# Ordering the first Winograd product by contraction chunk, and moving the second quad's four weight sums from VectorE to GpSimd

## The chip, the cores and the metric

The kernel runs on one core of a Trainium2 chip. The metric is the device time of one execution in microseconds. Three runs of the kernel before gave 762.72, 764.22 and 764.67, a median of 764.22 us.

The core's engines are TensorE (matmuls; PE in the profile, its weight loads PEld), VectorE (DVE), ScalarE (ACT), GpSimd (POOL) and SyncE (SP, which here only issues DMAs). Each engine has its own instruction stream and executes it in order; engines wait for each other and for DMAs through semaphores.

## The reference, cut to what matters

The kernel computes a transformer layer in float32: a cross-attention and a feed-forward part with low-rank experts, each with a residual. There are 16 batches of 64 tokens, so 1024 tokens, a model width of 512 and 32 heads of width 128. Only the key projection is touched:

```python
q = (hidden_q @ Wq).reshape(b, lq, h, dh)
k = (hidden_kv @ Wk).reshape(b, lk, h, dh)
v = (hidden_kv @ Wv).reshape(b, lk, h, dh)
score = jnp.einsum('bqhd,bkhd->bhqk', q, k) * scale + position_bias
...
return ctx @ Wo
```

`hidden_kv` is `ctx_4096` (1024 x 512) and `Wk` is 512 x 4096. The keys of four heads, 1024 x 512 numbers, are called a quad here; there are eight quads (`NQ`).

## The kernel before, in words

**Exact products.** A float32 operand is split into two parts that TensorE can take: `hi`, a rounded copy that ScalarE makes (L70, `nc.scalar.copy`, shown as CAST), and `lo`, the rest, which VectorE makes as source minus `hi` (L71, shown as TENSOR_TENSOR). A product is three matmuls, hi by hi, lo by hi and hi by lo (`mm3`, L256 to L260; in the profile all have L259). In the profile `gh` and `gl` are the two parts of a weight block, and `t1h`, `t1l`, `t6h` and so on those of a token block.

**Seven products instead of eight.** The projection of a quad is cut into 2 by 2 blocks (token half by model-width half against model-width half by column half) and done by Winograd's scheme with seven block products, numbered 1 to 7 and run in the order 1, 2, 6, 5, 7, 4, 3 (`ORDER`, L37). Product 1 multiplies plain blocks; product 6 multiplies a sum of weight blocks by a sum of token blocks; and so on.

- Weights (`class Weights`, L153 to L173) needs four sums of weight blocks, each one instruction over 128 x 512 numbers at L161: `s1` = a21 + a22 and `s2` = s1 - a11 when product 6 is prepared, `s3` = a11 - a21 for product 7, `s4` = a12 - s2 for product 3. The engine that makes them is an argument (`eng`). They come from a pool of four buffers (`sum`).
- Tokens (`class Tokens`, L119 to L146) needs four differences of token blocks, at L132, each in two instructions.

**One block product** has two column blocks (k = 0, 1), each of 128 columns and with its own PSUM bank, and a contraction of 256 in two chunks (kc = 0, 1) of 128. `mm_weights` (L262) does for one column block both chunks, six matmuls; the loop in `winograd` (L243 to L254) goes over the column blocks. After the last matmul of a column block, `post` evicts it or adds banks up: for product 1 a ScalarE copy `u` (L220), for product 2 a VectorE add `c` = `u` + PSUM bank (L223), and so on; a result block `c` is stored by SP (L340).

**The start of the program.** The first two quads, q = 0 and q = 1, go side by side (L363 to L399), because both need the same token blocks. For each product number, the code prepares quad 0's weights, the tokens and quad 1's weights, then does quad 0's and quad 1's product. SP loads what they need in the order of L299 to L309: the upper weight blocks and the first half of the tokens, by contraction chunk, come first; then the second half of the tokens; last the lower weight blocks a21 and a22 of quad 0 and of quad 1. Before the first real product, 18 small matmuls over zeros run on TensorE (L353). The operations ahead of the very first product are written out by hand (L354 to L361): chunk 0 of the tokens is split first, chunk 1 follows when its load is there.

**What sets the order.** TensorE's order is the order of the code (`manual_schedule`, L350). In this part of the program the order on VectorE, ScalarE, GpSimd and SP is set at build time by a planner, except for the lines L354 to L361. An order once set is fixed: an engine does not overtake a waiting instruction.

**What comes after.** At L400 to L408 the other key quads and the value products ("o" stages, `OctWeights`, four column blocks each, weight sums on VectorE at L193) follow; then queries and attention (L427 on), where GpSimd makes the query weights' sums (L430, L161) and adds the mask to the position bias (L461); then the feed-forward part. GpSimd also makes the token differences of the queries (L580, L132). The six banks of the PSUM pool `psp` and the two of `pss` are reused in turn, so a later product waits until an earlier one has been read out.

Of the kernel before, what the change touches and what calls it, by code (L numbers as in the profile page):

```python
# [36 lines left out]
ORDER = (1, 2, 6, 5, 7, 4, 3)  # L37
# [10 lines left out]
def xattn_ffn_kernel(ctx: ExitStack, tc: tile.TileContext, x, ctxT, wq, wk, wv, wo, fside, mask,  # L48
                     base_wT, base_b, arT, router_b, lora_b, expert_map, out):
    nc = tc.nc  # L50
# [12 lines left out]
    def bank(k=None):  # L63
        return psp.tile([P, 512], F32, tag="ps", name="ps")

    def blk(tag, name, dt=F32, shape=(P, 512)):
        return pools[tag].tile(list(shape), dt, tag=tag, name=name)
# [41 lines left out]
    with ExitStack() as actx:  # L109
# [6 lines left out]
        def small_bank(name):  # L116
            return pss.tile([P, 512], F32, tag="s", name=name)
# [92 lines left out]
                    self.make(i)  # L210
                return self

        def winograd(mm, n, emit, yzbank=bank, order=ORDER):

            xb, zb, yb, u, u2, u3 = ({} for _ in range(6))

            def post(i, k):
                if i == 1:
                    u[k] = blk("sn", "u")
                    nc.scalar.copy(u[k], xb[k])  # L220
                elif i == 2:
                    c = blk("ob", "c11")
                    nc.vector.tensor_tensor(c, u[k], zb[k], ALU.add)  # L223
                    emit(0, 0, k, c)
                elif i == 6:
                    u2[k] = blk("sn", "u2")
                    copied[:] = [nc.scalar.copy(u2[k], xb[k])]
                elif i == 7:
                    u3[k] = blk("sn", "u3")
                    copied[:] = [nc.scalar.copy(u3[k], xb[k])]  # L230
                    c = blk("ob", "c22")
                    nc.vector.tensor_tensor(c, u3[k], yb[k], ALU.add)
                    emit(1, 1, k, c)
                elif i == 4:
                    c = blk("ob", "c21")
                    nc.scalar.copy(c, xb[k])
                    emit(1, 0, k, c)
                elif i == 3:
                    c = blk("ob", "c12")
                    nc.vector.tensor_tensor(c, u2[k], yb[k], ALU.add)  # L240
                    emit(0, 1, k, c)

            for i in order:  # L243
                for k in range(n):
                    if i == 1:
                        xb[k] = bank()
                    elif i == 2:
                        zb[k] = yzbank(k)
                    elif i == 5:
                        yb[k] = yzbank(k)  # L250
                    b = xb if i in (1, 6, 7, 4) else zb if i == 2 else yb
                    mm(i, k, b[k], i in (1, 2, 5))
                    post(i, k)
                yield i  # L254

        def mm3(o, stat, mov, first, last):  # L256
            (sh, sl), (mh, ml) = stat, mov
            for n, (a, b) in enumerate(((sh, mh), (sl, mh), (sh, ml))):
                nc.tensor.matmul(o, lhsT=a, rhs=b, start=first and n == 0, stop=last and n == 2,  # L259
                                 skip_group_check=True)  # L260

        def mm_weights(t, g):  # L262
            def mm(i, k, o, first):
                for kc in range(2):
                    mm3(o, [a[:, kc, k * P:(k + 1) * P] for a in g[i]], [b[:, kc] for b in t[i]],
                        first and kc == 0, kc == 1)
            return mm
# [15 lines left out]
        def gran4(r, eng):  # L283
            return Weights(r[0, 0], r[0, 1], r[1, 0], r[1, 1], 256, eng)
# [8 lines left out]
        rks = {}, {}  # L293
# [44 lines left out]
        def emit_k(q):  # L338
            def emit(i, j, k, c):
                stored[:] = [nc.sync.dma_start(out=kd[4 * q + 2 * i + k][:, j * HALF:(j + 1) * HALF], in_=c)]  # L340
            return emit
# [4 lines left out]
            return emit  # L346

        tc_ = Tokens(cT, nc.vector)
        gs = [gran4(r, nc.vector) for r in rks]
        with tc.manual_schedule(engines={nc.tensor.engine}):  # L350
            warm = small_bank("warm")
            for _ in range(WARM):
# [1 line left out]
            with tc.manual_schedule(engines={nc.tensor.engine, nc.vector.engine, nc.scalar.engine}):  # L354
# [5 lines left out]
                nc.vector.tensor_tensor(lo[:, 0], cT[:, 0, 0:HALF], hi[:, 0].bitcast(F32), ALU.subtract)  # L360
                split(hi[:, 1], lo[:, 1], cT[:, 1, 0:HALF])  # L361
            gs[1].make(1)
            both = [winograd(mm_weights(tc_, gs[q]), 2, emit_k(q), yz) for q, yz in  # L363
                    enumerate((bank, lambda k: small_bank("yz")))]

            def keys_of(q, g):
                xn = {}
                for i in winograd(mm_weights(tc_, g), 2, emit_k(q)):
                    if 3 <= q < 7:
                        t = 2 * (q - 3)  # L370
                        if i in (1, 6):
                            xn[i] = x_tile(t + (i == 6))
                        if i in (6, 7):
                            with tc.issue_after(copied[-1].ins):
                                norm(sm, *([a] for a in xn[1 if i == 6 else 6]))
                        elif i == 5:
                            x_turn(t, xn[1][0])
                        elif i == 3:
                            x_turn(t + 1, xn[6][0])
# [20 lines left out]
            for n, (q, kind) in enumerate(stages[:-1]):  # L400
                load(n + 2)
                ops[n + 1].all()
                if kind == "k":
                    keys_of(q, ops[n])
                else:
                    for i in winograd(mm_oct(tc_, ops[n]), 4, emit_oct(q),
                                      lambda k: bank() if k < 2 else small_bank("yz")):
                        pass  # L408
                if n == 1:
                    with tc.issue_after(stored[-1].ins):  # L410
                        nc.sync.dma_start(out=m8, in_=mask)
                        nc.sync.dma_start(out=emi, in_=expert_map.partition_broadcast(P))
                        nc.sync.dma_start(out=rb, in_=router_b.partition_broadcast(P))
                    nc.vector.tensor_scalar(maskb, m8, -1.0, BIG, ALU.add, ALU.mult)
                    nc.vector.tensor_reduce(valid, m8, AX.X, ALU.max)
                    nc.vector.tensor_copy(emf, emi)
                    for e in range(E):
                        nc.vector.tensor_scalar(oneh[:, e, :], emf, float(e), 2.0, ALU.is_equal, ALU.mult)
# [188 lines left out]
            for p in range(NP):  # L607
                steps = ("QSQQQQQQt" if p == 0 else "SQQQPQQOOQOhOQOOOO" if p + 2 < NP else
                         "SQQQPQQOQQfSeeOOOOOhh" if p + 1 < NP else "PooOOOOOOO")
                n = 0  # L610
# [130 lines left out]
    def mm(o, a, b, start=False, stop=False):  # L741
        nc.tensor.matmul(o, lhsT=a, rhs=b, start=start, stop=stop, skip_group_check=True)  # L742
# [8 lines left out]
    def ffn_route(pa):  # L751
        lg = fs2.tile([P, NR], F32, tag="lg", name="lg")
        nc.vector.tensor_tensor(lg, pa[:, E * R:NAR], rb, ALU.add)
        nm = fs2.tile([P, 1], F32, tag="nm", name="nm")
        nc.vector.tensor_reduce(nm, lg, AX.X, ALU.max, negate=True)
        sme = fs2.tile([P, 1], F32, tag="sme", name="sme2")
        nc.scalar.activation(lg, lg, AF.Exp, bias=nm, accum_out=sme)
        return pa, lg, sme
# [58 lines left out]
    with tc.manual_schedule(engines=fixed):  # L817
# [10 lines left out]
        r = ffn_route(pas[0])  # L828
# [3 lines left out]
    with tc.manual_schedule(engines=fixed | {nc.vector.engine}):  # L832
        for t in range(NT):
# [4 lines left out]
            if t + 1 < NT:  # L838
                r = ffn_route(pas[t + 1])
            n = 1 if t else 2  # L840
# [55 lines left out]
```

## Time and profile before

| what | value |
|---|---|
| median of three runs | 764.22 us (762.72 to 764.67) |
| the profiled execution, span from first to last instruction | 761.7 us |
| mean granted TensorE clock in it | 0.999 |
| instructions | 16780 |
| the first matmul of the key projection | 4.73 us |
| first GpSimd instruction behind the making of constants | 111.88 us |

The profile is of one execution, and the page gives no time of its own for it besides the span. The median of the runs lies 2.5 us above the span; what lies around the span belongs to a run's time and not to the profile.

The views used below are these. The page's first part gives each engine's busy time and share of the span. The chain of waits is followed back from the last instruction, at each step to what released it. The list of waits tells which engine and line waited for which, with total, number and longest. A timeline has, for each instruction, the start, the length in us, the engine, the line, the operation, output `<-` inputs with shapes, and in square brackets the idle time ahead of it and what ended that. A VectorE instruction is listed with its full length, and the next one may start a little before that length is over, so that instructions 0.60 us apart are listed with 0.68. A table of windows has, for each stretch, its length, the busy time of PE, PEld, DVE, ACT and POOL with the number of instructions, the granted clock (PEclk), the busy share of the DMA engines and GB/s.

### The profile page before, as it was taken

What the parts mean: (1) busy time and instruction counts of PE and PEld (TensorE: products, weight loads), DVE (VectorE), ACT (ScalarE), POOL (GpSimd) and SP (SyncE); (2) the same over time, 40 slices, a digit from 0 to 9 for tenths busy, and PEclk for the clock granted to TensorE, in tenths of its full rate; (3) what the DMA queues carried; (4) which work ended last, traced back from release to release, by engine and by line L of the source; (5) the groups of instructions that cost most, each with busy time, mean ns of one, the idle gap of its engine ahead of it and who ended that gap; (6) DMA issues with size and microseconds to landing.
All of it is one profiled execution on the core that took longest, in us unless ns stands there. A gap on an engine that the chain in (4) does not pass through costs nothing.

```text
span 761.7 us, 16780 instructions
## 1 busy us (share of the span) xinstructions
PE 752.5 (99%) x6154; PEld 624.9 (82%) x6154; DVE 565.8 (74%) x1076; ACT 412.0 (54%) x1157; POOL 194.8 (26%) x271
## 2 busy tenths in 40 slices
PE   8999999999999999999999999999999999999998
PEld 6888888888788888877888888888888888888898
DVE  7986567666655776869778777787778777878975
ACT  5654444444444445667645565456645765474361
POOL 0000008108820693223220222022211232010330
PEclk9999999999999999999999999999999999999999
DMA  6685647465735446466554465436544564462011
GB/s 255 229 285 186 205 157 229 147 218 179 224 130 187 156 126 225 142 222 217 189 158 149 138 199 167 142 120 201 174 141 134 180 185 140 125 199 84 1 57 56
DMA packets 84946, 126.79 MB, mean 166 GB/s; under 512 B 11776, under 2 KB 35072, under 8 KB 84864
## 3 DMA queue, kind: packets, MB, share of 16 engines
q1 hardware_dynamic: 80624, 123.56, 49.9%
q0 software_dynamic: 4096, 2.11, 1.2%
q8 instruction: 48, 0.79, 0.5%
q14 instruction: 34, 0.28, 0.1%
q10 hardware_dynamic: 144, 0.06, 0.0%
HBM read 83.74 MB, written 35.65 MB: 157 GB/s over the span
## 4 chain that ended last, share of the span: by engine, by line
PE 91%; DVE 3%; POOL 2%; DMA 2%; issue 1%; ACT 0%; SPq 0%; DVEq 0%; ACTq 0%; POOLq 0%
PE ps L259 73%; PE yz L259 5%; PE ps L742 5%; PE ps L517 4%; PE pss L470 4%; POOL xT L333 1%; DMA cT<-in_ctxT 1%; DMA so<-in_wo 0%; DMA xT<-xb 0%; DVE bs L708 0%; DVE gl L71 0%; PE pt L104 0%; DVE s L161 0%; DVE ol L71 0%; POOL st L711 0%
## 5 line engine op out<-in xcount | busy, mean ns | idle before, releaser
L481 ACT ACTIVATE p<-p,nm 128x64 f32<-128x64 f32 x256 | 85.9, 339 | 33.3 <-DVE nm L475 31.0
L534 DVE TENSOR_TENSOR acc<-acc,ps 128x512 f32<-128x512 f32 x128 | 86.8, 681 | 21.2 <-PE ps L259 20.4
L259 PE MATMUL ps<-wh,ol 128*128 128x512 f32 x256 | 99.9, 390 | 0.8 <-DVE ol L71 0.8
L259 PE MATMUL ps<-wh,oh 128*128 128x512 f32 x256 | 100.1, 391 | 0.0
L259 PE MATMUL ps<-wl,oh 128*128 128x512 f32 x256 | 99.7, 389 | 0.0
L70 ACT CAST gh<-s 128x512 fp32r<-128x512 f32 (+1 forms) x128 | 64.4, 514 | 56.0 <-PE ps L259 45.7
L333 POOL DMA_DIRECT2D xT<-xb x128 | 69.7, 552 | 84.9 <-DVE xb L330 80.7
L71 DVE TENSOR_TENSOR gl<-s,gh 128x512 fp32r<-128x512 f32 (+1 forms) x128 | 72.0, 566 | 23.2 <-ACT gh L70 23.1
L161 POOL TENSOR_TENSOR s<-rq 128x256 f32<-128x256 f32 x32 | 25.3, 790 | 238.9 <-DMA rq<-in_wq 190.1
L71 DVE TENSOR_TENSOR ol<-ps,oh 128x512 fp32r<-128x512 f32 x64 | 39.9, 683 | 31.5 <-ACT oh L70 31.3
L70 ACT CAST gh<-raw 128x512 fp32r<-128x512 f32 x48 | 29.8, 623 | 52.8 <-PE yz L259 36.1
L259 PEld LDWEIGHTS ps<-wh,ol 128*128 128x128 f32 x256 | 48.1, 188 | 11.4 <-DVE ol L71 1.6
L259 PEld LDWEIGHTS ps<-wl,oh 128*128 128x128 f32 x256 | 48.1, 188 | 10.0
L259 PEld LDWEIGHTS ps<-wh,oh 128*128 128x128 f32 x256 | 48.0, 188 | 10.0
L71 DVE TENSOR_TENSOR gl<-raw,gh 128x512 fp32r<-128x512 f32 x48 | 35.1, 731 | 27.9 <-ACT gh L70 20.7
L461 POOL TENSOR_TENSOR bm<-bm,maskb 128x512 f32<-128x512 f32 x32 | 42.4, 1348 | 36.6 <-DMA bm<-in_fside 36.6
L481 ACT ACTIVATION_READ_ACCUMULATOR p<-p,nm 128x1 f32 x256 | 48.6, 190 | 0.0
L565 DVE TENSOR_TENSOR q<-u,ps 128x512 f32<-128x512 f32 x48 | 32.8, 683 | 20.4 <-PE ps L259 16.0
L70 ACT CAST oh<-ps 128x512 fp32r<-128x512 f32 x64 | 33.2, 590 | 11.0 <-PE ps L517 11.0
L70 ACT CAST gh<-rq 128x256 fp32r<-128x256 f32 x48 | 19.5, 406 | 36.0 <-PE ps L259 32.1
L517 PEld LDWEIGHTS ps<-pt,v 64*64 64x64 f32 x2048 | 31.9, 135 | 5.7 <-issue 5.6
L554 ACT COPY u<-ps 128x512 f32<-128x512 f32 x48 | 27.9, 581 | 15.9 <-PE ps L259 8.8
(258 smaller groups left out, 1986.2 us busy)
## 6 DMA issues: line engine op xcount, KB each, us to landing
kd<-c SPq DMA_DIRECT2D x64, 256.0 KB, 2.6
vd<-c SPq DMA_DIRECT2D x64, 256.0 KB, 2.8
kT<-kd SPq DMA_DIRECT2D x64, 256.0 KB, 3.9
v<-vd SPq DMA_DIRECT2D x64, 256.0 KB, 3.7
raw<-in_wk SPq DMA_DIRECT2D x32, 256.0 KB, 4.0
raw<-in_wv SPq DMA_DIRECT2D x32, 256.0 KB, 4.3
rq<-in_wq SPq DMA_DIRECT2D x32, 256.0 KB, 4.1
bm<-in_fside SPq DMA_DIRECT2D x32, 256.0 KB, 4.5
```

The lines of the kernel that those rows point to most:

```text
L70: first = nc.scalar.copy(hi, src)
L71: return first, (lo_eng or nc.vector).tensor_tensor(lo, src, hi.bitcast(F32), ALU.subtract)
L259: nc.tensor.matmul(o, lhsT=a, rhs=b, start=first and n == 0, stop=last and n == 2, skip_group_check=True)
L333: nc.gpsimd.dma_start(out=dst[32 * j:32 * j + 32, :, 32 * i:32 * i + 32], in_=xb[32 * i:32 * i + 32, j])
L461: nc.gpsimd.tensor_tensor(bm, bm, maskb, ALU.add)
L470: nc.tensor.matmul(ps[a * S:(a + 1) * S, t, :], lhsT=qT[n // 8][:, cq], rhs=kT[m // 8][:, ck], start=True, stop=True)
L481: nc.scalar.activation(p[:, t, :], p[:, t, :], AF.Exp, bias=nm[:, t:t + 1], accum_out=sme[:, t:t + 1])
L517: nc.tensor.matmul(ps[a][d:d + S, t * S:(t + 1) * S], lhsT=v[t // 2][r, t % 2, c], rhs=pt[r, :, t, :], start=True, stop=True)
L534: return nc.vector.tensor_tensor(acc[:, t, :], acc[:, t, :], ps, ALU.add)
L554: copy = nc.scalar.copy(s[i], b["x"])
L565: add = nc.vector.tensor_tensor(self.blocks[key], s[u], b[bk], ALU.add)
L742: nc.tensor.matmul(o, lhsT=a, rhs=b, start=start, stop=stop, skip_group_check=True)
```

## The change

There are two edits. First, for quad 0 alone, product 1 no longer finishes column block 0 before it begins column block 1: it does chunk 0 for both column blocks, then chunk 1 for both, and only then evicts both. `mm_weights` takes the chunk as an optional argument. Second, the `Weights` object of quad 1 gets GpSimd as the engine of its sums, so four instructions of L161 leave VectorE for GpSimd. Quad 0 keeps VectorE, and so do all later key quads.

```diff
-        def winograd(mm, n, emit, yzbank=bank, order=ORDER):
+        def winograd(mm, n, emit, yzbank=bank, order=ORDER, halves=False):
...
             for i in order:
+                if i == 1 and halves:
+                    for k in range(n):
+                        xb[k] = bank()
+                    for half in range(2):
+                        for k in range(n):
+                            mm(i, k, xb[k], True, half)
+                    for k in range(n):
+                        post(i, k)
+                    yield i
+                    continue
                 for k in range(n):
                     if i == 1:
                         xb[k] = bank()
...
         def mm_weights(t, g):
-            def mm(i, k, o, first):
-                for kc in range(2):
+            def mm(i, k, o, first, half=None):
+                for kc in range(2) if half is None else (half,):
                     mm3(o, [a[:, kc, k * P:(k + 1) * P] for a in g[i]], [b[:, kc] for b in t[i]],
                         first and kc == 0, kc == 1)
...
-        gs = [gran4(r, nc.vector) for r in rks]
+        gs = [gran4(r, e) for r, e in zip(rks, (nc.vector, nc.gpsimd))]
...
-            both = [winograd(mm_weights(tc_, gs[q]), 2, emit_k(q), yz) for q, yz in
+            both = [winograd(mm_weights(tc_, gs[q]), 2, emit_k(q), yz, halves=q == 0) for q, yz in
                     enumerate((bank, lambda k: small_bank("yz")))]
```

The number of matmuls and of all other instructions with work stays the same. The compiled programs differ in the order that the planner gives VectorE, ScalarE and SP in the first 50 us, which follows from the edits.

## The prediction

> **What bounds the kernel now.** First the page's busy shares and its chain of waits (shares of the span by engine):
>
> ```profile
> PE 752.5 (99%) x6154; PEld 624.9 (82%) x6154; DVE 565.8 (74%) x1076; ACT 412.0 (54%) x1157; POOL 194.8 (26%) x271
> PE 91%; DVE 3%; POOL 2%; DMA 2%; issue 1%; ACT 0%; SPq 0%; DVEq 0%; ACTq 0%; POOLq 0%
> ```
>
> TensorE carries nearly all of it, and the change leaves its 6154 matmuls as they are. So the change can only move the moments at which TensorE stands still. Both edits act in the first two quads of the key projection, so the next view is who TensorE waited for in the first 30 us (total us, times, longest):
>
> ```profile
> PE warm L353 <- DVE zero L84: 1.1, 1, 1.1
> PE ps L259 <- ACT t1h L70: 0.7, 1, 0.7
> PE ps L259 <- DVE gl L71: 0.4, 1, 0.4
> ```
>
> The timeline of TensorE shows both holes (start, length, engine, line, operation):
>
> ```profile
> 5.77 0.65 PE L259 MATMUL ps<-t1l,gh 128*128 128x512 f32 x1
> 7.12 0.50 PE L259 MATMUL ps<-t1h,gh 128*128 128x512 f32 x1 [0.70 <-ACT t1h L70]
> ...
> 17.73 0.39 PE L259 MATMUL ps<-t6h,gh 128*128 128x512 f32 x1
> 18.48 0.50 PE L259 MATMUL ps<-t6h,gl 128*128 128x512 f32 x1 [0.36 <-DVE gl L71]
> ```
>
> The first hole is at 6.4: chunk 0 of the tokens is used up and chunk 1 is not there. The second is at 18.1: product 6 of the first quad lacks the low half of its weight sum. In order of time, the chain is DMA, ACT and then DVE from 3.06 to 18.44, and nothing but TensorE from 18.48 to 167.96. So whatever delays the matmul at 18.48 goes into the end time one for one. Its releaser's engine:
>
> ```profile
> 14.74 0.68 DVE L161 TENSOR_TENSOR s<-raw 128x512 f32<-128x512 f32 x1
> 15.35 0.68 DVE L71 TENSOR_TENSOR t6l<-tt,t6h 128x512 fp32r<-128x512 f32 x1
> 15.95 0.68 DVE L161 TENSOR_TENSOR s<-s,raw 128x512 f32<-128x512 f32 x1
> 16.55 0.68 DVE L161 TENSOR_TENSOR s<-raw 128x512 f32<-128x512 f32 x1
> 17.15 0.68 DVE L223 TENSOR_TENSOR c<-u,ps 128x512 f32<-128x512 f32 x1
> 17.75 0.68 DVE L71 TENSOR_TENSOR gl<-s,gh 128x512 fp32r<-128x512 f32 x1
> ```
>
> VectorE works without a gap, one instruction each 0.60 us, and the `gl` at 17.75, done at 18.43, lets TensorE go on.
>
> **Part one, the first product by chunks.** Between 6.4 and 7.1 TensorE now does the three chunk-0 matmuls of the second column block. The three chunk-1 matmuls at 7.12, 7.46 and 7.84 keep their times (the third waits for the `t1l` that VectorE ends at 7.79), and after them 3 instead of 6 are left: 3 x 0.23 = 0.69 us gained at 8.9. The evictions `u` have room: ScalarE takes them in the old order, the first at 9.72, and both banks are full by 8.9. Product 2 then starts at 11.60 instead of 12.29, behind its last input `t2l` (done 10.54). TensorE comes to product 6 at 17.73 - 0.69 = 17.04. There it needs `gl`.
>
> **Part two, VectorE's order.** One would expect the `gl` to move forward, since the first sum of the second quad (16.55) leaves VectorE. The compiled order says otherwise. Before, behind the first quad's second sum (15.95), came that foreign sum, one output add (L223) and `gl`. After, come two output adds and `gl`. The second add has merely taken the place of the sum, and its operands are long there (its matmuls end near 14.6). So `gl` stays third, at 17.75. By itself this part gains nothing, and then part one gains nothing either: TensorE waits 0.69 longer for the same `gl`. Sum so far: 0.
>
> **Part three, GpSimd beside VectorE.** The first sum on GpSimd waits for the second quad's lower two weight blocks, which by the trace's landing records are there at 14.46 and 15.15. GpSimd is free since 2.4, so it starts at about 15.2, while VectorE is in the sum of 14.74. The second follows from its own result. What do the two engines do to each other? The trace has the pair once, at 273 us, where GpSimd makes token differences of the same shape:
>
> ```profile
> 273.24 3.35 POOL L132 TENSOR_TENSOR tt<-xT 128x512 f32<-128x512 f32 x2 [1.53 <-ACT gh L70]
> ```
>
> ```profile
> 273.05 0.69 DVE L71 TENSOR_TENSOR gl<-s,gh 128x512 fp32r<-128x512 f32 x1 [2.91 <-ACT gh L70]
> 273.66 1.78 DVE L71 TENSOR_TENSOR gl<-raw,gh 128x512 fp32r<-128x512 f32 x1
> 275.36 1.78 DVE L161 TENSOR_TENSOR s<-raw,s 128x512 f32<-128x512 f32 x1
> ...
> 281.70 1.27 DVE L232 TENSOR_TENSOR c<-u,ps 128x512 f32<-128x512 f32 x2
> ```
>
> GpSimd came 0.19 us after a VectorE instruction had begun; that one kept its 0.69, but the next two took 1.78, 1.10 more than 0.68, one for each GpSimd instruction. Both read two operands from SBUF. The two `c<-u,ps`, which read one operand from PSUM, took 1.27 together and lost nothing. A GpSimd instruction of this shape takes 1.28 at the least (the bias adds of L461), about 1.67 in this stretch.
>
> Applied here: the sum of 14.74 ends undisturbed at 15.4; GpSimd runs to about 16.6; `t6l`, due at 15.35, lasts 1.78 to 17.13. GpSimd's second sum stands ready at about 16.7 and goes next, to about 18.3; VectorE's second sum, handed on at 17.05, lasts 1.78 to 18.83. ScalarE makes `gh` from 18.86 to 19.48 (0.62, as at 16.66). The two output adds read PSUM and run at 18.75 and 19.35; `gl` starts at 19.95 and ends at 20.63. TensorE's first product-6 matmul runs at 19.5 and the second at 20.68 instead of 18.48: **+2.2 us** (2 x 1.10). Bounds: 0 if the two miss each other, 2 x 1.67 = 3.3 if VectorE stood still for the whole of both.
>
> [...]
>
> **What is late next.** The other two sums come later, once their buffers are free, and cost VectorE 1.10 each; two VectorE sums of 0.60 are gone by then. The low half of product 7's tokens is done at 27.08 and used at 29.29, product 4's at 31.3 and 34.73, and the whole chain moves with TensorE, so 2.2 and 3.4 us cover them. Without this cover each would cost up to 1.10. The output adds of product 3 that free PSUM banks move back up to nine places, 5.4 us: the second ended at 47.84, the bank is wanted at 52.58, and TensorE itself comes 2.2 later, so some 1.5 us are left. SP's loads are reordered by a few places; those used first (38.35, 43.54) no longer stand behind all the stores, so I cost this at nothing. GpSimd's next old work is at 111.88.
>
> **The clock.** TensorE would stand from 17.2 to 19.5 and, after one matmul, to 20.68. Does the granted clock hold? The windows of the profile (span, length, busy PE, PEld, DVE, ACT, POOL, then PEclk):
>
> ```profile
> 190.43:193.85 3.42, 2.23 (x10) 1.50 (x8) 1.20 (x6) 1.71 (x4) 1.96 (x4) 1.00 0.26 82
> 757.05:760.46 3.41, 1.38 (x9) 1.17 (x7) 0.75 (x2) 0.00 (x0) 0.00 (x0) 1.00 0.29 103
> 760.46:761.70 1.24, 0.00 (x0) 0.00 (x0) 0.00 (x0) 0.00 (x0) 0.00 (x0) 0.50 0.00 0
> ```
>
> 2.23 busy of 3.42 left it at 1.00; after 1.38 of 3.41 it was 0.50. The stretch 16.35 to 19.77 would have about 1.1 busy, less than the second. Bounds: nothing, or half rate for as long as at the start (from 1.05 to about 6.1, where 256 columns took 0.22 each and later 512 take 0.23), of which half, 2.5, is lost. I take 0.9: about an even chance of a stretch of 3.4 us at half rate, 1.7 lost.
>
> [...]
>
> **Sum.** 0 + 2.2 + 0.9 = +3.1 us. The profiled execution has a span of 761.7; the median of the three runs, 764.22, lies 2.5 above it, which I take as constant. **764.2 + 3.1 = 767.3 us.**
>
> **Rivals.** *One collision only*: if the load lands after 15.35, `t6l` passes first, GpSimd's first sum delays only VectorE's second sum, and its second falls beside the PSUM adds: +1.1, 765.3. For it: the margin is 0.2 us. Against: both engines follow the same loads. *Nothing changes*: GpSimd gets out of VectorE's way and `gl` stays at 17.75: 764.2. Against: the rows at 273. *Faster, the other side*: if `gl` came one place earlier, at 17.15, TensorE would go on at about 17.85 and 0.6 would be won; if the two holes vanished altogether, 0.69 + 0.52 = 1.2, down to 763.0. It decides only if something ahead of 14.74 gets quicker on VectorE; the compiled order there is the same instruction by instruction. *Worse*: a bank or a load is late at 50 us, or the clock falls for its longest: 769 and more.
>
> **Numbers.** 0.3% (2.3 us) is about what a measurement of this kernel can tell from no change. Two collisions 62%, one 14%, nothing 13%, faster 5%, worse 6%. The range from 764.0 to 769.0 leaves out the faster case, about half of "nothing" and most of "worse". Slower by over 0.3% means over 766.5: "worse" and most of the forecast, 58%. Even the full gain of 1.2 would lie within 0.3%: faster 4%, the same 38%.
>
> **What would show it.** Right: no wait for `t1h` at 6.4; a GpSimd sum at 15.2; `t6l` and the sum behind it at 1.78 each; the second product-6 matmul near 20.7, with TensorE waiting for ACT `gh` about 2.3 and for DVE `gl` about 0.9; perhaps a PEclk below 1.00 near 20 us; from there on the old timeline, shifted. Wrong: VectorE's instructions at 0.68 between 15 and 18, or `gl` before 17.75, or a new TensorE wait between 25 and 60.

## The result and the profile after

| | before | after |
|---|---|---|
| median of 13 runs each | 763.62 us (762.72 to 765.78) | 765.78 us (764.31 to 767.14) |
| span of the profiled execution | 761.7 us | 765.1 us (its run: 766.9) |
| mean granted TensorE clock | 0.999 | 1.000 |

The ratio is 1.0027, with a 95% interval of 1.0019 to 1.0035: 2.2 us slower, against a forecast of +3.1. The direction and the range held. The step that made up most of the forecast did not.

Busy shares and the chain of waits, after:

```profile
PE 753.9 (99%) x6154; PEld 625.6 (82%) x6154; DVE 562.9 (74%) x1072; ACT 410.9 (54%) x1157; POOL 201.4 (26%) x275
PE 87%; DVE 4%; DMA 3%; POOL 3%; issue 2%; ACT 1%; SPq 0%; DVEq 0%; ACTq 0%; POOLq 0%
```

The four sums have moved (DVE x1076 to x1072, POOL x271 to x275). TensorE's share of the chain falls from 91% to 87%. At the start, its stretch without a wait in the chain now begins at 34.99 instead of 18.48. Whom TensorE waited for in the first 60 us (total, times, longest):

```profile
PE warm L363 <- DVE zero L84: 1.0, 1, 1.0
PE ps L269 <- DVE gl L71: 0.6, 1, 0.6
PE ps L269 <- ACT u L230: 0.3, 1, 0.3
PE ps L269 <- ACT gh L70: 0.2, 1, 0.2
```

The hole at 6.4 us (`t1h`, 0.7) is gone in this profile. The one at 18 is 0.6 + 0.2 instead of 0.4. A new one has come, for an eviction `u`. TensorE's timeline has the three, and below them product 4 as it was before:

```profile
17.15 0.50 PE L269 MATMUL ps<-t6h,gh 128*128 128x512 f32 x1 [0.23 <-ACT gh L70]
18.30 0.50 PE L269 MATMUL ps<-t6h,gl 128*128 128x512 f32 x1 [0.64 <-DVE gl L71]
...
34.99 0.50 PE L269 MATMUL ps<-t4h,gh 128*128 128x512 f32 x1 [0.31 <-ACT u L230]
```

```profile
34.73 0.39 PE L259 MATMUL ps<-t4h,gh 128*128 128x512 f32 x1
```

The second matmul of product 6 is 0.18 us earlier than before (18.48), not 2.2 later. The first of product 4 is 0.26 later (34.73 before), and at 45 us, after more small gaps, TensorE is 0.41 late. Between 32 and 45 us it has lost 0.62. It stays 0.4 late to 300 us. In this execution more is lost further on, 0.9 us between 300 and 490 us and 1.95 near 497, so the last matmul is 3.38 us late; the difference of the two spans, 765.1 and 761.7, is not all an effect of the first 50 us. GpSimd and VectorE near 15 us, timelines:

```profile
15.30 2.29 POOL L161 TENSOR_TENSOR s<-raw 128x512 f32<-128x512 f32 x1 [12.92 <-DMA raw<-in_wk]
17.67 1.72 POOL L161 TENSOR_TENSOR s<-s,raw 128x512 f32<-128x512 f32 x1
```

```profile
15.16 0.68 DVE L71 TENSOR_TENSOR t6l<-tt,t6h 128x512 fp32r<-128x512 f32 x1
15.76 0.69 DVE L161 TENSOR_TENSOR s<-s,raw 128x512 f32<-128x512 f32 x1
16.36 1.28 DVE L223 TENSOR_TENSOR c<-u,ps 128x512 f32<-128x512 f32 x2
17.56 0.68 DVE L71 TENSOR_TENSOR gl<-s,gh 128x512 fp32r<-128x512 f32 x1
```

The two do collide here, but it is GpSimd's instruction that is lengthened. Its sum takes 2.29 instead of 1.28 and ends 1.23 us after VectorE has come to an instruction that reads PSUM (16.36). No VectorE instruction is longer than 0.69. Further on the other engine pays; GpSimd's third and fourth sums, and VectorE beside them:

```profile
23.31 1.61 POOL L161 TENSOR_TENSOR s<-raw 128x512 f32<-128x512 f32 x1 [3.92 <-DVE gl L71]
28.57 1.67 POOL L161 TENSOR_TENSOR s<-raw,s 128x512 f32<-128x512 f32 x1 [3.64 <-DVE gl L71]
```

```profile
23.69 2.38 DVE L132 TENSOR_TENSOR tt<-cT 128x512 f32<-128x512 f32 x2
...
29.01 1.78 DVE L71 TENSOR_TENSOR gl<-raw,gh 128x512 fp32r<-128x512 f32 x1
```

Here the two sums cost VectorE 1.10 each (2.38 for two instead of 1.28, and 1.78 instead of 0.68), as the rows at 273 us had it. The quad 0 sum `s4`, a VectorE instruction behind them, comes at 33.12. What ScalarE makes of it, and below it ScalarE before:

```profile
33.83 0.62 ACT L70 CAST gh<-s 128x512 fp32r<-128x512 f32 x1 [1.79 <-DVE s L161]
34.36 0.58 ACT L230 COPY u<-ps 128x512 f32<-128x512 f32 x1
34.84 0.62 ACT L70 CAST gh<-s 128x512 fp32r<-128x512 f32 x1
35.36 1.07 ACT L230 COPY u<-ps 128x512 f32<-128x512 f32 x2
```

```profile
30.85 0.59 ACT L230 COPY u<-ps 128x512 f32<-128x512 f32 x1 [0.34 <-PE ps L259]
32.27 0.59 ACT L230 COPY u<-ps 128x512 f32<-128x512 f32 x1 [0.83 <-PE ps L259]
33.14 0.62 ACT L70 CAST gh<-s 128x512 fp32r<-128x512 f32 x1 [0.27 <-DVE s L161]
```

This is the new wait. In the changed program's order on ScalarE, the conversion `gh` of quad 0's fourth sum (VectorE's) stands ahead of all four evictions `u` of product 7, and that of quad 1's (GpSimd's) ahead of the last three. Those evictions free the banks that product 4 writes. Before, two `u` ran ahead of the first conversion, the first at 30.85; now the first `u` stands behind the first `gh` until 34.36. The conversion is needed only for product 3, after 40 us.

### The profile page after: what moved, and what is told of

The parts are those of the page before. It is cut to its first block, busy times and chain, and to the rows that moved or that the text cites. A ratio compares the mean times of both kernels' runs of the same rounds, so it can differ in the third digit from the quotient of the medians.

```text
span 765.1 us, 16781 instructions
## 1 busy us (share of the span) xinstructions
PE 753.9 (99%) x6154; PEld 625.6 (82%) x6154; DVE 562.9 (74%) x1072; ACT 410.9 (54%) x1157; POOL 201.4 (26%) x275
## 4 chain that ended last, share of the span: by engine, by line
PE 87%; DVE 4%; DMA 3%; POOL 3%; issue 2%; ACT 1%; SPq 0%; DVEq 0%; ACTq 0%; POOLq 0%
PE ps L269 69%; PE ps L752 5%; PE yz L269 5%; PE ps L527 4%; PE pss L480 3%; POOL xT L343 2%; DMA raw<-in_wk 1%; DMA rq<-in_wq 1%; DVE gl L71 1%; ACT p L491 1%; POOL s L161 1%; DVE tt L132 0%; DVE bs L718 0%; PE pt L104 0%; DVE acc L544 0%
## 5 line engine op out<-in xcount | busy, mean ns | idle before, releaser
L71 DVE TENSOR_TENSOR gl<-s,gh 128x512 fp32r<-128x512 f32 (+1 forms) x128 | 73.6, 579 | 26.6 <-ACT gh L70 26.5
L161 POOL TENSOR_TENSOR s<-rq 128x256 f32<-128x256 f32 x32 | 25.5, 796 | 239.9 <-DMA rq<-in_wq 211.8
```

Of the source, the lines that this page charges most:

```text
L71: return first, (lo_eng or nc.vector).tensor_tensor(lo, src, hi.bitcast(F32), ALU.subtract)
L161: self.eng.tensor_tensor(r, a, b, op)
```

## The experiments

Two theories were set against each other first: that the GpSimd sums cost the time (first pair, `s1` and `s2`, or second pair, `s3` and `s4`), or that the chunk order does (A and B in the expectations; A1 and A2 are the early and the late pair). Later the question was by which way, and whether early at all (P and Q). "Late at 72 us" is the start of the same TensorE matmul (number 300, at 71.45 in the profile of before) in each version's profile, less its start in before. "Lost at 32 to 45" is the part of it that comes between these two times. The two "pauses" are gaps of TensorE near 372 and 497 us, in the attention part, in which it waits for nothing that the list of waits shows ("issue"); the one profile of before has neither.

| version | late at 72 us | lost at 32 to 45 us | pause at 372 / 497 us | median, before beside it | ratio (95%) |
|---|---|---|---|---|---|
| after | +0.41 | 0.62 | 1.0 / 1.7 | 765.78, 763.62 | 1.0027 (1.0019 to 1.0035) |
| after again | +1.18 | 1.09 | 0.5 / 0 | 764.89, 763.75 | 1.0025 (1.0006 to 1.0045) |
| chunks only | -0.04 | 0.0 | 0.7 / 1.7 | 764.57, 763.94 | 1.0006 (0.9989 to 1.0023) |
| sums only | +0.87 | 1.08 | 0.8 / 1.2 | 765.20, 763.94 | 1.0021 (1.0005 to 1.0037) |
| late pair on GpSimd | -0.28 | 0.0 | 0.7 / 1.3 | 765.15, 763.94 | 1.0019 (1.0003 to 1.0035) |
| the same again | -0.15 | 0.0 | 1.2 / 0 | 763.53, 764.21 | 0.9985 (0.9970 to 1.0000) |
| early pair on GpSimd | +0.27 | 0.0 | 0.7 / 0 | 764.12, 763.94 | 0.9995 (0.9977 to 1.0014) |
| `s4` on VectorE | +0.33 | 0.0 | 1.0 / 2.0 | 764.57, 764.21 | 1.0011 (0.9991 to 1.0031) |
| memsets for sums | -0.35 | 0.0 | 1.0 / 1.7 | 763.82, 763.75 | 0.9995 (0.9985 to 1.0005) |
| `gh` behind `u` | +0.01 | 0.0 | 0.8 / 0 | 764.52, 763.75 | 1.0005 (0.9991 to 1.0020) |
| the same again | +0.15 | 0.0 | 0 / 0 | 764.15, 764.21 | 0.9999 (0.9987 to 1.0012) |
| late second sum | +12.37 | 0.0 | 0.2 / 2.0 | 777.06, 764.21 | 1.0165 (1.0148 to 1.0182) |

**Parts of the change.** Chunk order alone, all sums on VectorE:

```diff
-        gs = [gran4(r, e) for r, e in zip(rks, (nc.vector, nc.gpsimd))]
+        gs = [gran4(r, nc.vector) for r in rks]
```

> The first product goes by chunks as in the change, the second quad's sums stay on VectorE. VectorE's order is then that of the kernel before, so its gl for product 6 ends near 18.3 as before. Theory A (the loss comes from GpSimd's sums and the orders they bring with them): the second product-6 matmul at 18.3 to 18.5, product 4 at 34.7 as before, and the time within 0.7 us of the kernel before. Theory B (the chunk order itself costs, for example by later evictions): 1.5 to 2.5 us slower, with a shift that shows before 60 us.

The hole at 6.4 us is down to 0.3 us (0.32, at 7.2), `gl` is third as before, and nothing is gained or lost that can be measured. GpSimd's sums alone, without the chunk order:

```diff
-            ... emit_k(q), yz, halves=q == 0) for q, yz in
+            ... emit_k(q), yz, halves=False) for q, yz in
```

> The second quad's four sums go to GpSimd, the first product is done as before. Theory A: the chain from GpSimd's second sum (ends near 19.4) through VectorE and ScalarE's waiting gh to product 4 sets the time, so TensorE reaches product 4 near 35.0 and the time is that of the changed kernel, 1.5 to 2.5 us above the kernel before. Theory B: within 0.7 us of the kernel before.

About as slow as the whole change. TensorE reaches product 4 at 34.52, not near 35.0, but waits 0.79 us within it, at 36.83, for an eviction `u`; GpSimd's fourth sum took 7.10 us here. So by the traces the sums are the part that costs; the intervals of the two times overlap. Then the sums by pairs, late (`s3`, `s4`) and early (`s1`, `s2`) ones (in these versions `summed` picks the engine by the sum's name, a line not shown):

```diff
-        gs = [gran4(r, e) for r, e in zip(rks, (nc.vector, nc.gpsimd))]
+        gs = [gran4(r, e) for r, e in zip(rks, (nc.vector, dict(s1=nc.vector, s2=nc.vector, s3=nc.gpsimd, s4=nc.gpsimd)))]
```

> As the changed kernel, but the second quad's sums s1 and s2 (product 6) are made by VectorE, s3 and s4 (products 7 and 3) by GpSimd. Here ScalarE's first u copy of product 7 stands ahead of the gh of s4. Theory A1 (it is GpSimd's late first pair, which VectorE waits 1.2 us for through gh): the time is that of the kernel before, product 4 at 34.7. Theory A2 (it is the two collisions of the second pair at 23 and 29 us, 1.1 us each on VectorE): as the changed kernel, 1 to 2 us above the kernel before.

```diff
-        gs = [gran4(r, e) for r, e in zip(rks, (nc.vector, nc.gpsimd))]
+        gs = [gran4(r, e) for r, e in zip(rks, (nc.vector, dict(s1=nc.gpsimd, s2=nc.gpsimd, s3=nc.vector, s4=nc.vector)))]
```

> As the changed kernel, but s1 and s2 of the second quad are made by GpSimd and s3 and s4 by VectorE. Theory A1: the loss is that of the changed kernel, 1 to 2 us above the kernel before, with VectorE idle for 1.2 us near 19. Theory A2: VectorE has no collision after 20 us, product 4 starts at 34.7 or earlier and the time is that of the kernel before within 0.7.

The early pair costs nothing that can be measured, although GpSimd's first sum takes 2.62 us there and VectorE later stands 1.23 us for the second. The late pair seemed to cost 1.2 us (medians), but its profile shows nothing late at 72 us, which did not fit.

**The changed kernel again.**

> The changed kernel once more, for a second profile. Two theories of the 2.2 us. (P) The loss is early: TensorE waits at product 4 (35 us) since ScalarE's conversions of the GpSimd sums stand ahead of the evictions u of product 7. P expects the wait of 0.6 to 1.3 us at product 4 again, TensorE 0.3 to 0.5 us late at 72 us, and then that the rest of the 2.2 us is scatter: repeated times nearer to +1 than to +2. (Q) The loss is late: pauses of TensorE at 372 and 497 us in which it waits for nothing the profile shows, 1.0 and 1.2 to 1.7 us. If Q is bound to the program, both pauses are back in this profile and the time is again 1.5 to 2.5 us over before; if they come and go with the execution, one of them can be absent and they are no reason for a difference in the median.

The second profile shows another course. GpSimd's fourth sum, ScalarE, and TensorE:

```profile
28.86 7.10 POOL L161 TENSOR_TENSOR s<-raw,s 128x512 f32<-128x512 f32 x1 [3.64 <-DVE gl L71]
```

```profile
35.99 0.62 ACT L70 CAST gh<-s 128x512 fp32r<-128x512 f32 x1 [1.85 <-POOL s L161]
36.51 1.07 ACT L230 COPY u<-ps 128x512 f32<-128x512 f32 x2
```

```profile
37.14 0.50 PE L269 MATMUL ps<-t4h,gh 128*128 128x512 f32 x1 [0.80 <-ACT u L230]
```

This time GpSimd's sum was the one lengthened. VectorE ran ten instructions with both operands in SBUF one after the other, each 0.60 us behind the last, and the sum ended at 35.96, 1.24 us after VectorE's first instruction that reads PSUM (34.72). The conversion waited for it, the eviction behind it too, and TensorE lost 0.80 within product 4 and was 1.18 late. So one program has two courses by whose instruction is lengthened near 28.8: 0.62 or 1.09 us are lost between 32 and 45 us. (The other 0.3 of the difference at 72 us is already there at 20 us.) The version with the sums only, with its fourth sum of 7.10, lost 1.08 there. The theory of a loss bound to fixed late pauses falls: the pause at 497 is absent here. Whether the repeated time is nearer to +1 or to +2 is not clear: the medians differ by 1.14, the ratio says 1.9.

**Memsets in place of the sums.** GpSimd writes the same tiles but reads nothing; the orders on VectorE and ScalarE stay those of the changed kernel.

```diff
-                self.eng.tensor_tensor(r, a, b, op)
+                if self.eng is nc.gpsimd and self.cols == 256:
+                    self.eng.memset(r, 0.5)
+                else:
+                    self.eng.tensor_tensor(r, a, b, op)
```

> As the changed kernel, but GpSimd's four sums are replaced by four memsets of the same tiles: GpSimd writes as much and reads nothing, waits for no load and no sum, and the orders on VectorE and ScalarE are those of the changed kernel. The second quad's weight sums are left out. Theory P (GpSimd's reading, beside VectorE and late for ScalarE) expects: no VectorE instruction of 1.78 us before 35 us, no wait at product 4, TensorE 0.2 us early at 72 us as in the version with late sums only, and a time within 1 us of before. The rival, that the new order alone costs it (planner's order on VectorE, ScalarE and SP), expects the wait at product 4 as in the changed kernel, +0.4 us at 72 us, and +2 us in time. Theory Q bound to the program expects about +2 us with nothing lost before 72 us.

No VectorE instruction is lengthened (none is over 0.69 between 14 and 37 us; the two memsets there took 0.53 each), no wait is left at product 4, TensorE is 0.35 early and the time is that of before. So the orders alone cost nothing; they cost only when a sum comes late. This profile has both late pauses at full length (1.0 and 1.7), and yet the median is that of before; the profiled run itself took 767.58.

**`gh` behind the evictions.** The sums stay on GpSimd; ScalarE's order is mended, for the weights of product 3. (VectorE's `gl` of these weights moves back with them, behind output adds.)

```diff
-                    gs[0].make(ORDER[n + 1])
+                    with tc.issue_after(copied[-1].ins) if ORDER[n + 1] == 3 else ExitStack():
+                        gs[0].make(ORDER[n + 1])
...
-                    gs[1].make(ORDER[n + 1])
+                    with tc.issue_after(copied[-1].ins) if ORDER[n + 1] == 3 else ExitStack():
+                        gs[1].make(ORDER[n + 1])
```

> As the changed kernel, but ScalarE converts the fourth sums of both quads only behind the four evictions u of product 7 (the sums stay on GpSimd). If the price is ScalarE's queue (head of line), the wait at product 4 goes, TensorE is 0.0 to 0.3 us early at 72 us although GpSimd's sums still lengthen VectorE's instructions near 23.7 and 29 us to 1.78, and the time is within 1 us of before. If the price is the lengthened VectorE instructions themselves (1.10 each), product 4 stays late by about 0.4 us and the time about +2 us. By theory Q nothing changes in the time: +2 us, with pauses at 372 and 497 us. A new wait at product 3 (near 40 us) would be this edit's own price.

> The version with ScalarE's conversions behind the evictions once more, since its first interval (0.9991 to 1.0020) leaves room for 1.5 us. If ScalarE's queue is the price, TensorE stands within 0.3 us of before at 72 us in the profile, whoever wins near 29 us (GpSimd's fourth sum of 1.6 or of 6.5 to 7.1 us), and the time is within 1 us of before. If GpSimd's late sums cost by another way, the time is again 1.5 to 2.5 us over before.

The two profiles happen to show both courses. The first has GpSimd's fourth sum at 6.50 us, the second this, with VectorE's instruction beside it lengthened:

```profile
28.95 1.67 POOL L161 TENSOR_TENSOR s<-raw,s 128x512 f32<-128x512 f32 x1 [3.64 <-DVE gl L71]
```

```profile
29.40 1.78 DVE L71 TENSOR_TENSOR gl<-raw,gh 128x512 fp32r<-128x512 f32 x1
```

In neither does TensorE wait between 30 and 60 us (the view of its waits is empty there), and it is 0.01 and 0.15 late. So the collisions near 24 (2.39 and 2.38 for two VectorE instructions) and the one at 29.40 are still there and cost TensorE nothing: the price is in ScalarE's queue. The times, 1.0005 and 0.9999 of before, agree, though the first interval reaches to 1.0020.

**`s4` alone back to VectorE.**

```diff
-                self.eng.tensor_tensor(r, a, b, op)
+                (nc.vector if name == 's4' and self.cols == 256 else self.eng).tensor_tensor(r, a, b, op)
```

> As the changed kernel, but the second quad's fourth sum is VectorE's; the first three stay on GpSimd. Theory: it is this one sum, and ScalarE's conversion of it, that comes late. Expected then: no wait of TensorE at product 4, TensorE 0.1 to 0.3 us early at 72 us or up to 0.3 late by the first pair, time within 1 us of before. Rival, that any late sum on GpSimd costs by lengthening VectorE's instructions near 23.7 us: TensorE late by 0.4 us or more at 72 us and time up by 1 to 2 us.

The wait at product 4 goes with the one sum; the 0.33 late are of the first 19 us (0.35 already at 18.84, in an execution in which GpSimd's first sum starts at 15.53 instead of 15.30). In time it lies between: 1.0011, and its interval holds both 1 and the ratio of the changed kernel. It speaks for the theory by its trace, not by its time.

**The late pair again.**

> The version with the third and fourth sums alone on GpSimd once more: its time was 1.0019 of before although its profile shows no loss at 72 us (GpSimd's fourth sum took 1.67 us there). By the theory of two outcomes, other executions have the long fourth sum (6.5 to 7.1 us), with a wait of TensorE for an eviction u between 35 and 38 us and 0.5 to 1.2 us lost: this profile may show it. Time 1 to 1.5 us over before. If the profile shows the short sum again and the time is over before again, something after 72 us is behind it.

The profile has the short fourth sum again (1.68), nothing is late at 72 us, and the time is 0.9985 this time. So the 1.0019 of the first series was most likely scatter, which its interval had not shown. Part of it is in the record: four of the 12 runs of the first series have a granted clock of 0.998 or 0.997 and took 766.99 to 768.91, and none of the 11 of the second has. In that version's order on ScalarE the first `u` of product 7 stands ahead of both conversions, and three of the four stand ahead of that of GpSimd's sum.

**A longer run of VectorE instructions.** The first output add of product 2 was put behind `gl` (early pair on GpSimd; the lines for that, and the one that keeps `low`, are not shown).

```diff
-                    nc.vector.tensor_tensor(c, u[k], zb[k], ALU.add)
+                    with tc.issue_after(gs[0].low[1].ins) if halves else ExitStack():
+                        nc.vector.tensor_tensor(c, u[k], zb[k], ALU.add)
```

> First pair of the second quad's sums on GpSimd (third and fourth on VectorE), and the first output add of quad 0's product 2 only behind the gl of its product 6. So VectorE runs sum, t5l, tt and gl, all with two operands from SBUF, where it had two output adds that read PSUM. If GpSimd gets in only when VectorE comes to an instruction that reads PSUM or waits (as its 7.10 us and 2.3 to 2.6 us suggest), the sum that starts at 15.3 ends about 18.4 or later (3.1 us or more, against 2.3 and 2.6), its second ends near 20.2 or later, and VectorE has no instruction over 0.70 before that. If instead the two take turns, the sum ends near 17 and one VectorE instruction lasts 1.78. gl itself stays about 17.6, so TensorE's product 6 of quad 0 gains nothing (18.3 to 18.5); quad 1's may wait.

GpSimd's sum and VectorE's first instruction with an operand from PSUM:

```profile
15.37 4.36 POOL L161 TENSOR_TENSOR s<-raw 128x512 f32<-128x512 f32 x1 [12.98 <-DMA raw<-in_wk]
```

```profile
18.50 0.68 DVE L224 TENSOR_TENSOR c<-u,ps 128x512 f32<-128x512 f32 x1
```

The sum ends at 19.73, again 1.23 after VectorE's PSUM instruction, and nothing on VectorE is over 0.70 before. Quad 1's product 6 waits, TensorE is 1.32 late at 72 us, and the single run took 765.41 (before 763.75).

**A known delay.** To learn whether an early loss goes into the time one for one, six more instructions between GpSimd's two sums (early pair on GpSimd):

```diff
+                    if isinstance(self.eng, dict):
+                        for _ in range(6):
+                            nc.gpsimd.tensor_scalar(self.s1, self.s1, 1.0, None, ALU.mult)
                     self.s2 = self.summed(self.s1, a11, ALU.subtract, "s2")
```

> A known delay, to read the scale: first pair on GpSimd, second pair on VectorE (the version whose time was 0.9995), and between GpSimd's first and second sum six multiplications by 1.0 of the first sum in place, so that the second sum, its conversion and quad 1's product 6 come later, by 3 to 8 us as an estimate from the 0.53 us of a GpSimd memset and the 1.28 of a GpSimd sum. If a wait of TensorE in the first 40 us goes into the end one for one, the measured time is over before by as much as TensorE is late at 72 us, within 1 us. If the time is up by clearly more (half as much again), early waits cost something further on too, and the 2.2 us of the changed kernel can come from an early loss of 0.4 to 1.2; if clearly less, some of the loss is made good later.

The six took 11.20 us, more than estimated. TensorE waited 9.80 us, was 12.37 late at 72 us, and the time rose by 12.85 (medians; 11.3 to 13.9 by the interval). It is one for one within that interval: nothing large is made good or multiplied.

## Why the prediction was right in the number and wrong in its main step

**Part one: right.** The hole at 6.4 is gone, product 2 starts at 11.32 (11.60 foretold), and TensorE is ready for product 6 at 16.92 (17.15 less its 0.23 of waiting; 17.04 foretold). This varies with the execution: in the second profile 0.17 us of the hole are left and product 2 starts at 11.88. Alone the part gains nothing measurable, 1.0006.

**Part two: right.** `gl` stayed third and came at 17.56; the 0.19 are VectorE's slightly earlier start.

**Part three: wrong.** The step that failed is "`t6l`, due at 15.35, lasts 1.78 to 17.13", and with it "VectorE's second sum ... lasts 1.78" and the +2.2 us. GpSimd did start at 15.30, 0.14 us into `t6l`, but VectorE kept 0.68 and 0.69, and GpSimd's sum took 2.29. The second product-6 matmul came at 18.30, not 20.68: -0.2 us where +2.2 stood. The price of 1.10 per collision was right, and was paid at 23.7 and 29.0; but the rows at 273 us show one of two outcomes, and I took it for the only one. (The pair was not there just once: VectorE's rows at 278.40 and 280.00, 1.68 and 1.78, show the same outcome.) What the rival "nothing changes" described, GpSimd getting out of VectorE's way, is what happened at 15. Two signs that the prediction named for being wrong came: VectorE at 0.68 between 15 and 18, and a new wait of TensorE between 25 and 60.

**What is late next: right for what it looked at, incomplete.** I covered the lengthened VectorE instructions by the low halves of the tokens: `t4l` had 3.4 us to spare, and the two runs with ScalarE's order mended show that this cover holds. I did not ask what ScalarE converts from the late sums, and what stands behind that conversion. The order of ScalarE could be read beforehand, as VectorE's was. The term costed at nothing measured 0.62 to 1.09 us, lost between 32 and 45 us. The output adds of product 3 and SP's loads made TensorE wait nowhere in the first 60 us, as foretold.

**The clock: wrong, since the stand did not come.** The 0.9 us did not come. In the first 60 us TensorE never stood more than 0.64 at a time behind its start, and the clock stayed at 1.00. With the known delay TensorE did stand. The windows around it (length, busy PE, PEld, DVE, ACT, POOL, PEclk, DMA, GB/s):

```profile
24.00:25.00 1.00, 0.00 (x0) 0.00 (x0) 0.00 (x0) 0.00 (x0) 0.92 (x2) 1.00 0.00 0
25.00:26.00 1.00, 0.00 (x0) 0.00 (x0) 0.00 (x0) 0.00 (x0) 1.00 (x1) 0.52 0.00 0
34.00:35.00 1.00, 1.00 (x4) 0.81 (x3) 1.00 (x3) 0.37 (x1) 0.00 (x0) 0.50 0.00 0
35.00:36.00 1.00, 1.00 (x6) 0.76 (x5) 1.00 (x3) 0.21 (x1) 0.00 (x0) 0.86 0.00 0
```

The last matmul before the wait ended at 21.57. The clock fell at about 25.04 (a mean of 0.52 over 25 to 26 leaves 0.04 us at full rate), 3.5 us later. It came back at about 35.28, 3.9 us after work was taken up at 31.36. Half the rate over 3.9 us is 2 us, which with 9.8 us of waiting is most of the 12.4.

The clock also fell after a shorter stand. In "chunks only" TensorE stood 1.73 us near 497 us, and after that the clock was down for 3.41 us ("memsets for sums", which stood 1.7 us there, has a mean clock of 0.998):

```profile
496.37:499.78 3.41, 1.68 (x38) 1.30 (x30) 1.57 (x3) 1.52 (x4) 2.32 (x2) 1.00 0.67 183
499.78:503.19 3.41, 3.41 (x10) 2.64 (x9) 2.21 (x4) 1.52 (x4) 0.00 (x0) 0.50 0.58 192
```

A pause as long was not always followed by a fall: in the first profile of the changed kernel it was 1.72 us, and the clock was 1.00 from 496 to 510 us. By the windows read, the clock fell after 1.38 busy of 3.41 us (757.05, before) and after 1.68 of 3.41 (496.37, "chunks only"), and stayed at 1.00 after 2.23 of 3.42 and 2.33 of 3.41 (190.43 and 337.21, before) and after 2.55 of 3.42 (16.35 to 19.77, the changed kernel's first profile). These are single stretches, and no limit was shown. The rows at 757 and 760 us were read rightly, and a stretch with the 1.1 busy of the forecast could have been one that a fall follows. What the term lacked is the stand. Its 3.4 us at half rate were an estimate; where the clock fell with work still to come, it was down for 3.41 us ("chunks only") and, by the times above, 10.24 us (known delay).

**The sum.** The forecast's +3.1 was 2.2 + 0.9 from two terms that both came out at about nothing, and the actual slowdown came from a term that I had put at nothing. That the number fits is luck.

**What is shown and what is open.** Shown by trace: TensorE's new wait at product 4, who it waits for, and that it goes when the sums read nothing, when `s4` alone is VectorE's, or when ScalarE's order is mended. Between 32 and 45 us the three profiles with that wait lose 0.62, 1.09 and 1.08, and the others nothing. The times say less. The three series with the wait have ratios of 1.0021 to 1.0027, and those without it, apart from the known delay, 0.9985 to 1.0019: no gap to speak of. By medians the three lie 2.2, 1.1 and 1.3 us above before, a mean of 1.5, and the eight without it between -0.7 and 1.2, a mean of 0.3. The difference of 1.2 fits the traced loss and a scale of one for one, but single series scatter by as much. Why the first series of the change lies at 2.2 is open. Two series of one program differ by as much (the late pair 1.0019 and 0.9985), and TensorE's pauses of up to 2.0 us at 372 and 497 us come and go between executions of the same program, so it may be scatter.

The forecast's base was the span plus 2.5 us, taken as constant. That difference mixes executions: in every later run a program's time lies 1.7 to 1.9 us above its own span. The sum does not change by it, since it starts from the median.

No version clearly beats the kernel before: the most that any profile shows won at 72 us is 0.35 us, less than these measurements can tell.

## What to carry to other kernels

When work moves to a slower engine, follow its result one engine further: list what stands behind its consumer in that engine's fixed order, since an early-issued conversion of a late result holds up evictions that have nothing to do with it (0.62 to 1.09 us lost here). A collision seen once in a trace is one outcome; price it for both engines, GpSimd's instruction lengthened as well as VectorE's. Where the effect is a few tenths of a percent, a known delay and a second series of the same program tell what the scale and the scatter are.

## What the runs showed of the hardware

- A GpSimd sum over SBUF beside VectorE instructions that read two SBUF operands had two outcomes, at the same phase. In the first profile of the changed kernel GpSimd started 0.16 us into a VectorE instruction (28.57 after 28.41), took 1.67 and lengthened the next one to 1.78. In the second it started 0.16 us into it too (28.86 after 28.70), took 7.10, and lengthened none. Of the seven profiles with that sum on GpSimd, in four it took about 1.67 and in three 6.50 to 7.10.
- Where GpSimd's sum was lengthened, it ended 1.22 to 1.24 us after the start of the next VectorE instruction that reads PSUM, however long it had taken: so in nine first and fourth sums that took over 2 us (2.29 to 7.10, in six profiles; VectorE's instruction was at 16.36, 18.50, 34.01, 34.41 and 34.72 for five of them). In the second profile of the changed kernel VectorE ran ten instructions back to back ahead of it, 6 us (28.70 to 34.72), and the GpSimd sum had begun before nine of them (28.86).
- There is a course between the two. In both profiles of the late pair VectorE paused before 25 us (0.17 us in the first, for ScalarE); the third sum took 2.88 there, and VectorE's next instruction 1.54 and 1.57.
- TensorE's pauses with nothing waited for stand near 372 and 497 us. The profile of before has neither. Of the 13 others 12 have the first (0.2 to 1.2 us) and seven the second (1.2 to 2.0). Packets of 16 KB run in a DMA queue that the profile calls "instruction" (48 in all). In the first profile of the changed kernel TensorE goes on at 499.43, 2.39 us after such a packet starts (497.04); in the profile of before, without the pause, one had started 4.32 us ahead of the same matmul (491.91 and 496.23). No run tests whether the packets have to do with the pauses.
